# Cross-attention in a decoder layer: each unit's products on 64 columns of the tensor engine put side by side

## The chip, the cores and the metric

The kernel runs on one core of a Trainium2 chip. The core has a tensor engine (PE, with its own weight loads, PEld), a vector engine (DVE), a scalar engine (ACT), GpSimd (POOL) and a queue engine that issues most DMAs (SP). Each engine works through its own instructions strictly in the order in which they stand in its queue; engines wait for each other by semaphores. The metric is the device time of one execution in microseconds, the median of the timed runs; lower is better.

## What is computed

The reference is one decoder layer on x of 16 x 64 tokens by 256, in float32: three blocks, each added to x after a LayerNorm. The first is self-attention with block-scaled four-bit weights, the third a mixture of 16 experts with a shared expert. The change lies in the second, cross-attention against a context of 16 x 64 x 64 (16 batches, 16 heads, keys and values kept as 64 latent values):

```python
q_hk  = (hidden_q @ Wq.T).reshape(B, S, H, K)              # H = 16 heads, K = 128
q_big = einsum('bshk,hkq->bshq', q_hk, w_kc_q)             # 192 wide
q_big = _apply_rope(q_big, sin_q, cos_q)                   # rotated queries
kv_r  = _apply_rope(kv_c, sin_k, cos_k)
q_r   = einsum('bshq,hqr->bhsr', q_big, W_qr)              # 64 wide
k_r   = einsum('bld,hdr->bhlr', kv_r, W_kr)
attn  = softmax(einsum('bhsr,bhlr->bhsl', q_r, k_r))
ctx_c = einsum('bhsl,bld->bhsd', attn, kv_r)               # 64 wide
ctx   = einsum('bhsd,hkd->bhsk', ctx_c, w_kc_kv)
out   = ctx.reshape(B, S, H * K) @ Wo.T
```

## The kernel before

Products of weights are folded ahead of use (the function quad_steps, four heads, a "quad", at a time): Wq with w_kc_q into w_q (L431), W_qr with W_kr into w_s (L453), w_kc_kv with Wo into w_o (L470). With these, cross-attention has four products for each unit. A unit is one quad of heads for one half (512) of the tokens, so there are eight of them, in the list units. For each unit:

1. rotated_queries is a generator with three steps, t0, t1 and t2. A step makes two tiles of 128x512 in PSUM by w_q, each of six products with split operands (L104, tiles mm<-xn,w_q). DVE multiplies each tile by two tables of the rotation (L980, rt), and POOL adds or subtracts the results (L986, roped, two per step).
2. pair_queries multiplies the six roped tiles by w_s (L1001). Each product uses 64 of the array's 128 columns; there are twelve, written into two tiles of PSUM, one for each pair of heads. ACT copies these to q_r (L1012). A float32 product shows as two passes in the trace, so twelve products are 24 passes.
3. pair_scores multiplies q_r of one pair with the context (L1024, eight products on 64 columns, kv_bd holds two heads' keys side by side) and starts softmax: DVE takes the maximum (L324), subtracts it (L326), ACT takes the exponential (L327), DVE sums and inverts (L329, L330), and POOL scales (L334, pn). For the last unit DVE scales too.
4. transposed turns pn on PE (L343) and ACT copies it to pt (L351, L352).
5. pair_context multiplies pt with the context (L1037, eight products on 64 columns for each pair); ACT and DVE split the result into c_t (L112, L113).
6. cross_project multiplies c_t by w_o (L104, mm<-w_o,c_t, four tiles of 128x256) and DVE adds the result to x (L1062).

The loop over n interleaves three units: in iteration n unit n is rotated (items 1), unit n-1 gets its queries and scores (2 and 3), and unit n-2 its context and projection (4 to 6). Folding of quads 2 and 3 (late, in iterations 1 and 3) runs between, and so do LayerNorm's transposes (L216) in iterations 0 and 6, the router's products (choose, L793 and L794), and in the last iteration the first products of the third block.

The order in an engine's queue is not that of the code. A scheduler takes the program in the code's order as a priority and places each instruction by its own estimate of when its operands are there, so that products of different steps come to stand between one another. Two means hold it: tc.issue_after(ins) and the helper after(...) put what is traced inside them behind a given instruction in the queue of its engine, without a wait; behind(read, writes) makes an instruction wait, by semaphore, for a list of others on other engines.

[...] The pool ps_mm gives four rotating tiles, which the rotated queries, pair_queries, the folding and cross_project share: a new tile waits until DVE or ACT has read the one four places before. Scores and transposes rotate over two tiles (at), contexts and others over two (av). roped tiles are single, rt tiles double.

Of the kernel before, what the change touches and what calls it, by code (L numbers as in the profile page):

```python
# [71 lines left out]
def decoder_layer(ctx: ExitStack, tc: tile.TileContext, a: dict, out: bass.AP):  # L72
    nc = tc.nc
# [11 lines left out]
    def mm_tile(rows=128, cols=512):  # L85
        return ps_mm.tile([128, 512], F32, tag="mm", name="mm")[:rows, :cols]
# [7 lines left out]
    @contextmanager  # L94
    def after(*instructions):

        with ExitStack() as order:
            for ins in instructions:
                order.enter_context(tc.issue_after(ins))
            yield  # L100

    def matmuls(ps, pairs):
        for n, (l, r) in enumerate(pairs):
            m = nc.tensor.matmul(ps, lhsT=l, rhs=r, start=(n == 0), stop=(n == len(pairs) - 1))  # L104
        return m.ins
# [143 lines left out]
    def behind(read, writes):  # L249
        for w in writes:  # L250
            tc.add_manual_dep(
                read,
                w.name,
                mybir.DependencyInfo(mybir.DependencyClass.Sync, mybir.DependencyReason.DATA),
                reason="it reads rows of each",
            )
# [58 lines left out]
    with ExitStack() as attn:  # L315
# [4 lines left out]
        def softmax(sc, scale, eng=None):  # L320

            shape = [128, 8, S]
            m = small.tile([128, 8], F32, tag="sm_m", name="sm_m")
            nc.vector.tensor_reduce(m, sc, AX.X, ALU.max)  # L324
            p = soft.tile(shape, F32, tag="p", name="p")
            nc.vector.tensor_tensor(p, sc, m.unsqueeze(2).broadcast_to(shape), ALU.subtract)  # L326
            exps.append(nc.scalar.activation(p, p, AF.Exp, scale=scale).ins)  # L327
            s = small.tile([128, 8], F32, tag="sm_s", name="sm_s")
            nc.vector.tensor_reduce(s, p, AX.X, ALU.add)  # L329
            nc.vector.reciprocal(s, s)  # L330
            pn = soft.tile(shape, F32, tag="pn", name="pn")
            softened.append(
                (eng or nc.vector)
                .tensor_tensor(pn, p, s.unsqueeze(2).broadcast_to(shape), ALU.mult)  # L334
                .ins
            )
            return pn
# [143 lines left out]
        weights, quad_loads = {}, []  # L481
# [9 lines left out]
        with tc.tile_pool(name="sw", bufs=2, side="right") as sw, tc.tile_pool(name="sa", bufs=2, side="right") as sa:  # L491
# [121 lines left out]
            vs, qks, pns, os = {}, {}, {}, {}  # L613
# [15 lines left out]
            for h in range(NH + 3):  # L629
# [9 lines left out]
                pt = transposed(pns.pop(h - 2)) if 0 <= h - 2 < NH else None  # L639
# [315 lines left out]
        with (  # L955
# [6 lines left out]
            def rotated_queries(w_q, half, roped):  # L962
                for t in range(3):
                    m = []
                    for ab in range(2):
                        ps = mm_tile()
                        cols = slice(t * 128, (t + 1) * 128)
                        pairs = []
                        for c in range(2):
                            pairs += three(  # L970
                                [w[:, c, ab, cols] for w in w_q],
                                [p[:, c, :] for p in xn_t[half]],
                            )
                        matmuls(ps, pairs)
                        ps3 = ps.rearrange("p (b s) -> p b s", s=S)
                        for k in range(2):
                            mt = xa.tile(
                                [128, 8, S], F32, tag=f"rt{ab}{k}", name=f"rt{ab}{k}"
                            )
                            nc.vector.tensor_tensor(mt, ps3, rope_table(t, 2 * ab + k), ALU.mult)  # L980
                            m.append(mt)
                    for ab, (one, two, op) in enumerate(
                        ((m[0], m[3], ALU.subtract), (m[2], m[1], ALU.add))
                    ):
                        r = xa.tile([128, 512], F32, tag=f"roped{t}{ab}", name=f"roped{t}{ab}", bufs=1)
                        nc.gpsimd.tensor_tensor(  # L986
                            r.rearrange("p (b s) -> p b s", s=S), one, two, op
                        )
                        roped.append(r)
                    yield  # L990

            def pair_queries(w_s, roped):
                ps = [mm_tile() for _ in range(2)]
                left = [4 if h in (1, 2) else 2 for h in range(4)]
                first = [True] * 4
                for t in range(3):
                    for ab in range(2):
                        for blk in range(2):
                            h = BLOCK_HEADS[t][blk]
                            left[h] -= 1  # L1000
                            nc.tensor.matmul(  # L1001
                                ps[h // 2][(h % 2) * 64 : (h % 2) * 64 + 64],
                                lhsT=w_s[:, t, blk, ab, :],
                                rhs=roped[2 * t + ab],
                                start=first[h],
                                stop=left[h] == 0,
                            )
                            first[h] = False
                q_rs = []
                for pr in range(2):  # L1010
                    q_r = xa.tile([128, 512], F32, tag="q_r", name="q_r", bufs=2)
                    nc.scalar.copy(q_r, ps[pr])  # L1012
                    q_rs.append(q_r)
                return q_rs

            def pair_scores(q_r, half, eng):

                sc = at_tile([128, 8, S])
                sc4 = sc.rearrange("p (h g) s -> p h g s", h=2)
                for g in range(2):  # L1020
                    for pp in range(2):
                        for par in range(2):
                            b = 4 * g + 2 * par + pp
                            nc.tensor.matmul(  # L1024
                                sc4[par * 64 : par * 64 + 64, :, 2 * g + pp, :],
                                lhsT=q_r[:, b * S : (b + 1) * S],
                                rhs=kv_bd[:, half * 8 + b],
                                start=True,
                                stop=True,
                            )  # L1030
                return softmax(sc, 1.0, eng)

            def pair_context(pt, half):
                av = av_tile()
                for k in range(4):
                    for hp in range(2):
                        nc.tensor.matmul(  # L1037
                            av[hp * 64 : hp * 64 + 64, k * 128 : (k + 1) * 128],
                            lhsT=kv[:, half * 4 + k, :],
                            rhs=pt[:, 4 * hp + k].rearrange("p a q -> p (a q)"),  # L1040
                            start=True,
                            stop=True,
                        )
                c_t = [
                    xa.tile([128, 512], F32R, tag=f"c_t{n}", name=f"c_t{n}", bufs=4)
                    for n in range(2)
                ]
                parts_of(av, c_t[0], c_t[1])
                return c_t

            def cross_project(w_o, c_ts, half, last):
                for k in range(4):
# [68 lines left out]
            units = [(0, 0), (1, 0), (0, 1), (2, 0), (3, 0), (1, 1), (2, 1), (3, 1)]  # L1121
            late = {1: quad_steps(2, weights, xb), 3: quad_steps(3, weights, xw)}
            prep = iter(())
            roped, pns = {}, {}
            for n in range(len(units) + 2):
                here = range(len(units))
                if n in late:
                    prep = late[n]
# [3 lines left out]
                rotate = iter(rotated_queries(weights[qd][0], half, roped[n]) if n in here else ())  # L1132
                pts_n = [transposed(pn) for pn in pns.pop(n - 2, ())]
                if n - 1 in here:
                    q_rs = pair_queries(weights[units[n - 1][0]][1], roped.pop(n - 1))
                c_ts = [pair_context(pt, units[n - 2][1]) for pt in pts_n]
                next(rotate, None)
                if n - 1 in here:

                    eng = nc.gpsimd if n < len(units) else nc.vector  # L1140
                    pns[n - 1] = [pair_scores(q_rs[0], units[n - 1][1], eng)]
                if n in late:
                    next(prep)
                next(rotate, None)
                if n == 0:
                    with tc.issue_after(highs[-1]), tc.issue_after(lows[-1]):
                        xn_t += layernorm_t(2, (1,))
                if n - 1 in here:
                    pns[n - 1].append(pair_scores(q_rs[1], units[n - 1][1], eng))
                if n in late:  # L1150
                    next(prep)
                if n - 2 in here:
# [364 lines left out]
```

## Time and profile before

| | us |
|---|---|
| median of 3 timed runs (lowest, highest) | 567.59 (567.42, 567.69) |
| the profiled execution, its own time | 574.92 |
| its span, first to last instruction | 573.2 |
| busy in the span: PE, PEld | 539.9, 446.9 |
| busy in the span: DVE, ACT, POOL | 402.5, 278.9, 229.6 |
| mean granted clock of PE | 0.978 |

In rows of the timeline the fields are start and length in us, engine, line, operation, tiles written and read, the part of the array (rows*columns for PE), shapes and count; in brackets stands the idle time of the engine before, with what ended it. The end of a matmul is modelled, and the next one starts before it: the pace of PE is read from starts. In windows each engine has its busy time in the stretch and its number of instructions, followed by the granted clock, the DMA share and GB/s.

### The profile page before, as it was taken

Reading aid. Unit: us, or ns where it says so; the run is one execution under the profiler, and the core shown is the slowest. Engines: PE = TensorE matmul, PEld = TensorE weight load, DVE = VectorE, ACT = ScalarE, POOL = GpSimd, SP = SyncE. Lnnn points to the kernel's source line nnn. Section 1 sums busy time; section 2 is a strip of 40 time slices with the busy share of each in tenths; the row PEclk is TensorE's granted clock in tenths of the full one; section 3 lists DMA queues with packets and bytes.
Section 4 is the critical chain, followed back from the end, with each engine's and each line's share of the span. In section 5 each row is a group of like instructions: output and inputs, shape, how many; then the busy total and the mean of one; then the engine's idle time right before and its main releaser. Section 6 shows DMA issues by size and latency. Waiting matters only on the chain.

```text
span 573.2 us, 10602 instructions
## 1 busy us (share of the span) xinstructions
PE 539.9 (94%) x4013; PEld 446.9 (78%) x4013; DVE 402.5 (70%) x879; ACT 278.9 (49%) x524; POOL 229.6 (40%) x213
## 2 busy tenths in 40 slices
PE   7999999999999989999999999999999869999962
PEld 6889898888989875757777577685787769999961
DVE  5465566645655789848667486889768589999876
ACT  4767557575574431230432323152535277777551
POOL 4260500101001005526244343632545726888872
PEclk9999999999999999999999999999999789999995
DMA  8563331823200599471020000000511667777384
GB/s 244 143 189 118 105 111 45 226 82 112 75 1 1 169 249 305 131 233 44 2 70 1 8 1 1 0 31 0 189 50 69 204 197 254 243 245 241 120 283 151
DMA packets 44262, 70.83 MB, mean 124 GB/s; under 512 B 11824, under 2 KB 25232, under 8 KB 44208
## 3 DMA queue, kind: packets, MB, share of 16 engines
q1 hardware_dynamic: 39376, 58.71, 34.3%
q0 software_dynamic: 3696, 10.36, 4.7%
q10 hardware_dynamic: 1136, 1.05, 0.6%
q8 instruction: 33, 0.54, 0.4%
q14 instruction: 21, 0.17, 0.1%
HBM read 48.61 MB, written 21.86 MB: 123 GB/s over the span
## 4 chain that ended last, share of the span: by engine, by line


## 5 line engine op out<-in xcount | busy, mean ns | idle before, releaser
L986 POOL TENSOR_TENSOR roped<-rt,rt 128x512 f32<-128x512 f32 x48 | 62.7, 1327 | 82.5 <-DVE rt L980 80.2
L980 DVE TENSOR_TENSOR rt<-mm,rope_q 128x512 f32<-128x512 f32 x96 | 61.5, 684 | 23.7 <-PE mm L104 23.0
L104 PE MATMUL mm<-xn,w_q 128*128 128x512 f32 x288 | 74.2, 403 | 0.5 <-ACT xn L222 0.5
L104 PEld LDWEIGHTS mm<-xn,w_q 128*128 128x128 f32 x288 | 52.1, 188 | 14.3 <-issue 2.6
L104 PE MATMUL mm<-xs,w 128*128 128x384 f32 x270 | 55.5, 355 | 6.2 <-ACT xs L112 5.1
L1300 POOL DMA_INDIRECT yd<-y,to x45 | 48.2, 1071 | 27.3 <-ACT y L1295 12.8
L104 PEld LDWEIGHTS mm<-xs,w 128*128 128x128 f32 x270 | 48.7, 199 | 8.1 <-ACT xs L112 5.9
L327 ACT ACTIVATE p<-p 128x512 f32<-128x512 f32 x32 | 20.1, 630 | 61.9 <-DVE p L326 61.9
L1001 PE MATMUL mm<-roped,w_s 128*64 128x512 f32 x192 | 46.3, 601 | 0.0
L324 DVE TENSOR_REDUCE sm_m<-at 128x8 f32<-128x512 f32 x32 | 21.8, 680 | 34.9 <-PE at L569 34.0
L514 POOL TENSOR_TENSOR wv<-code,scale 128x512 fp32r<-128x512 f32 x7 | 9.0, 1283 | 90.1 <-DMA scale<-in_scales 55.4
L609 DVE TENSOR_TENSOR x<-mm,x 128x256 f32<-128x256 f32 x64 | 26.0, 419 | 23.9 <-PE mm L104 22.7
L104 PE MATMUL mm<-wo,o 128*128 128x256 f32 x256 | 39.6, 295 | 0.0
L104 PE MATMUL mm<-xn,wk 128*128 128x512 f32 x128 | 35.3, 406 | 0.0
L104 PE MATMUL av<-w,hp 128*128 128x256 f32 x225 | 34.9, 289 | 0.3 <-ACT y L1295 0.3
L104 PE MATMUL mm<-wv,xn 128*128 128x256 f32 x256 | 34.7, 288 | 0.0
L586 PE MATMUL av<-pt,v 128*128 128x128 f32 x256 | 34.5, 277 | 0.0
L104 PE MATMUL mm<-xn,wq 128*128 128x512 f32 x128 | 34.4, 404 | 0.0
L104 PEld LDWEIGHTS mm<-wo,o 128*128 128x128 f32 x256 | 32.9, 190 | 1.5 <-issue 0.4
L586 PEld LDWEIGHTS av<-pt,v 128*128 128x128 f32 x256 | 32.0, 191 | 1.2
L104 PEld LDWEIGHTS mm<-wv,xn 128*128 128x128 f32 x256 | 31.7, 189 | 0.7
L104 PEld LDWEIGHTS av<-w,hp 128*128 128x128 f32 x225 | 30.3, 189 | 1.3 <-ACT y L1295 0.6
(216 smaller groups left out, 1148.7 us busy)
## 6 DMA issues: line engine op xcount, KB each, us to landing
w<-in_W SPq DMA_DIRECT2D x15, 640.0 KB
code<-in_codes SPq DMA_DIRECT2D x32, 256.0 KB
scale<-in_scales SPq DMA_DIRECT2D x32, 256.0 KB
xr<-xd SPq DMA_DIRECT2D x15, 408.0 KB
xd<-zeros SPq DMA_DIRECT2D x8, 720.0 KB
yd<-zeros SPq DMA_DIRECT2D x8, 512.0 KB
got<-yd SPq DMA_DIRECT2D x16, 256.0 KB
wq<-in_Wq SPq DMA_DIRECT2D x4, 512.0 KB
```

The costliest lines, as they stand in the source:

```text
L104: m = nc.tensor.matmul(ps, lhsT=l, rhs=r, start=(n == 0), stop=(n == len(pairs) - 1))
L324: nc.vector.tensor_reduce(m, sc, AX.X, ALU.max)
L327: exps.append(nc.scalar.activation(p, p, AF.Exp, scale=scale).ins)
L514: mults[n] = eng.tensor_tensor(w, *loaded[gr].pop(n), ALU.mult).ins
L586: nc.tensor.matmul(av[:, k * 128 : (k + 1) * 128], lhsT=v[:, i, k0 : k0 + HD], rhs=pt[:, i].rearrange("p a q -> p (a q)"), start=True, sto ...
L609: nc.vector.tensor_tensor(x[i], ps, x[i], ALU.add)
L980: nc.vector.tensor_tensor(mt, ps3, rope_table(t, 2 * ab + k), ALU.mult)
L986: nc.gpsimd.tensor_tensor(r.rearrange("p (b s) -> p b s", s=S), one, two, op)
L1001: nc.tensor.matmul(ps[h // 2][(h % 2) * 64 : (h % 2) * 64 + 64], lhsT=w_s[:, t, blk, ab, :], rhs=roped[2 * t + ab], start=first[h], stop=l ...
L1300: sent = nc.gpsimd.indirect_dma_start(out=yd[: (E - 1) * SLOTS + min(TOPK, E - 1 - e) * NT], out_offset=bass.IndirectOffsetOnAxis(ap=to[:, ...
```

## The change

One unit's products on 64 columns are put in one row of PE's queue: the twelve of pair_queries, then the contexts of both pairs of the unit ahead, then the scores of both pairs. For that:

- rotated_queries yields the last product of the step, and pair_queries, pair_context and pair_scores return theirs; each next group is traced inside after(...) of the last product of the one before.
- The first step (t0) of unit n now comes ahead of pair_queries of unit n-1; the second (t1) comes behind the scores of both pairs.
- roped_last keeps the last two rotations traced; their list is passed by roped_done, and the first product of pair_queries waits for both (behind), where before each product waited for its own operand alone.
- The folding steps of late quads move behind the scores.

No product, copy or DMA is added or left out. In the lines of the changed file L1001 becomes L1004, L1012 becomes L1017, L1024 becomes L1029, L1037 becomes L1042, and L1062 becomes L1067.

```diff
@@ rotated_queries
-                        matmuls(ps, pairs)
+                        asked = matmuls(ps, pairs)
...
-                        nc.gpsimd.tensor_tensor(
+                        rotated = nc.gpsimd.tensor_tensor(
                             r.rearrange("p (b s) -> p b s", s=S), one, two, op
                         )
                         roped.append(r)
-                    yield
+                        roped_last[ab] = rotated.ins
+                    yield asked
@@ pair_queries
-                            nc.tensor.matmul(
+                            products.append(
+                                nc.tensor.matmul(
...
+                behind(products[0], roped_done.pop())
...
-                return q_rs
+                return q_rs, products[-1]
@@ pair_scores, pair_context: the last product is returned too
-                return softmax(sc, 1.0, eng)
+                return softmax(sc, 1.0, eng), last.ins
...
-                return c_t
+                return c_t, last.ins
@@ the loop over units
+            roped_last, roped_done = [None, None], []
             for n in range(len(units) + 2):
...
                 pts_n = [transposed(pn) for pn in pns.pop(n - 2, ())]
                 if n - 1 in here:
-                    q_rs = pair_queries(weights[units[n - 1][0]][1], roped.pop(n - 1))
-                c_ts = [pair_context(pt, units[n - 2][1]) for pt in pts_n]
-                next(rotate, None)
+                    roped_done.append(list(roped_last))
+                order = [m for m in [next(rotate, None)] if m]
                 if n - 1 in here:
-
-                    eng = nc.gpsimd if n < len(units) else nc.vector
-                    pns[n - 1] = [pair_scores(q_rs[0], units[n - 1][1], eng)]
-                if n in late:
-                    next(prep)
-                next(rotate, None)
+                    with after(*order):
+                        q_rs, product = pair_queries(
+                            weights[units[n - 1][0]][1], roped.pop(n - 1)
+                        )
+                    order = [product]
+                c_ts = []
+                for pt in pts_n:
+                    with after(*order):
+                        c_t, product = pair_context(pt, units[n - 2][1])
+                    order = [product]
+                    c_ts.append(c_t)
                 if n == 0:
                     with tc.issue_after(highs[-1]), tc.issue_after(lows[-1]):
                         xn_t += layernorm_t(2, (1,))
                 if n - 1 in here:
-                    pns[n - 1].append(pair_scores(q_rs[1], units[n - 1][1], eng))
+
+                    eng = nc.gpsimd if n < len(units) else nc.vector
+                    pns[n - 1] = []
+                    for q_r in q_rs:
+                        with after(*order):
+                            pn, product = pair_scores(q_r, units[n - 1][1], eng)
+                        order = [product]
+                        pns[n - 1].append(pn)
+                if n in late:
+                    next(prep)
+                with after(*order):
+                    next(rotate, None)
                 if n in late:
                     next(prep)
                 if n - 2 in here:
```

More of the change, by code (lines that the diff above doesn't have):

```diff
@@ L989, in rotated_queries @@
                         roped.append(r)
-                    yield
+                        roped_last[ab] = rotated.ins
+                    yield asked
             def pair_queries(w_s, roped):
-                ps = [mm_tile() for _ in range(2)]
+                ps, products = [mm_tile() for _ in range(2)], []
                 left = [4 if h in (1, 2) else 2 for h in range(4)]
@@ L1000, in pair_queries @@
                             left[h] -= 1
[L1001 to L1006, printed above, removed]
+                            products.append(
+                                nc.tensor.matmul(
+                                    ps[h // 2][(h % 2) * 64 : (h % 2) * 64 + 64],
+                                    lhsT=w_s[:, t, blk, ab, :],
+                                    rhs=roped[2 * t + ab],
+                                    start=first[h],
+                                    stop=left[h] == 0,
+                                ).ins
                             )
                             first[h] = False
+                behind(products[0], roped_done.pop())
                 q_rs = []
@@ L1023, in pair_scores @@
                             b = 4 * g + 2 * par + pp
-                            nc.tensor.matmul(
+                            last = nc.tensor.matmul(
                                 sc4[par * 64 : par * 64 + 64, :, 2 * g + pp, :],
@@ L1036, in pair_context @@
                     for hp in range(2):
-                        nc.tensor.matmul(
+                        last = nc.tensor.matmul(
                             av[hp * 64 : hp * 64 + 64, k * 128 : (k + 1) * 128],
```

## The prediction

> **What bounds the kernel now.** I read the page first (span, busy time by engine, slices), then the windows by stage, then the tensor engine's timeline through one unit of the stage that the change touches, then the waits, and last the stretches behind it where the tensor engine pauses.
>
> ```profile
> span 573.2 us, 10602 instructions
> PE 539.9 (94%) x4013; PEld 446.9 (78%) x4013; DVE 402.5 (70%) x879; ACT 278.9 (49%) x524; POOL 229.6 (40%) x213
> ...
> PEclk9999999999999999999999999999999789999995
> ```
>
> The profiled execution took 574.92 us, 1.7 more than its span; the median of the timed runs is 567.59. I sum differences against the profiled one and carry them over unchanged. What a measurement of this kernel can tell from no change is about 0.2%, 1.1 us.
>
> ```profile
> 336.00:358.00 22.00, 22.00 (x160) 15.57 (x159) 16.35 (x29) 7.40 (x12) 11.13 (x9) 1.00 0.01 1
> ```
>
> The columns are stretch, length, then busy time of PE, PEld, DVE, ACT and POOL. In cross-attention (about 214 to 419 us) PE has work without a break while VectorE is busy three quarters and GpSimd half of the time: PE's queue sets the pace. Busy PE is not all products, though, as one unit shows:
>
> ```profile
> 335.36 3.13 PE L104 MATMUL mm<-w_o,c_t 128*128 128x256 f32 x24
> 338.32 2.96 PE L104 MATMUL mm<-xn,w_q 128*128 128x512 f32 x12
> 341.21 3.71 PE L1001 MATMUL mm<-roped,w_s 128*64 128x512 f32 x16
> 344.85 0.66 PE L343 MATMUL at<-ident,pn 128*128 128x128 f32 x4
> 345.26 1.64 PE L104 MATMUL mm<-xn,w_q 128*128 128x512 f32 x6
> 346.74 0.60 PE L343 MATMUL at<-ident,pn 128*128 128x128 f32 x4
> 347.10 2.35 PE L104 MATMUL mm<-xn,w_q 128*128 128x512 f32 x9
> 349.37 1.94 PE L1001 MATMUL mm<-roped,w_s 128*64 128x512 f32 x8
> 351.14 1.92 PE L1037 MATMUL av<-pt,kv 128*64 128x128 f32 x32
> 352.88 1.04 PE L1024 MATMUL at<-kv_bd,q_r 128*64 128x128 f32 x16
> 353.86 2.37 PE L104 MATMUL mm<-xn,w_q 128*128 128x512 f32 x9
> 356.16 1.09 PE L1024 MATMUL at<-kv_bd,q_r 128*64 128x128 f32 x16
> ```
>
> Each row gives start, length, source line, tiles and the part of the array used: 128*64 are the products on 64 columns. They stand in three groups here (from 341.21, 349.37 and 356.16), with 128-column work between.
>
> **The saving.** The cost of one excursion to 64 columns, from these rows: twelve xn passes at 0.233 ((2.96 less the last pass's 0.40, over 11) are 2.80, but 338.32 to 341.21 is 2.89: 0.09 on entering. The L1024 group entered from 128 columns takes 1.09, the one entered from 64 columns 1.04: 0.05. That group lasts 0.98 to the next start (352.88 to 353.86), where 16 of the 32 L1037 passes take 0.87 (1.74 / 2): 0.11 on leaving. And the xn group right behind takes 0.1 longer (331.33 to 334.33 is 3.00 against 2.89). Sum 0.35 us. The waits say the same of the weight loads:
>
> ```profile
> PEld mm L1001 <- issue: 20.5, 73, 0.4
> ```
>
> Counted in the timeline there are 34 such groups between 223 and 412 us; in the changed program's PE queue 16 remain: one for each of the eight iterations with queries, three split again (four w_q products of L431 come between the first unit's queries and scores, eight transposes in iteration 7, L793 and L794 twice in iteration 8), three for the weight steps L453 and L470, one for the last context. 18 x 0.35 = **6.3 us saved**. No product is added or dropped; the DMA issues on SP's queue keep their order.
>
> **What is moved, and what it now waits for.** PE's queue becomes, per unit: t1 (second of three rotations, 12 xn passes a pair of tiles), w_o x18 (passes of L104), transposes A, w_o x6, t2, t0 of the next unit, transposes B, 24 L1001 passes, 32 context, 32 score, all in order. Before, the first 16 L1001 passes needed only t0 and t1, and stood in PE's queue as cover while VectorE and GpSimd rotated t2. Now the explicit wait holds even the first L1001 for the last rotated tile; queued behind it are contexts, scores, the next t1, and with them VectorE's softmax. The cover left is t0 of the next unit (2.8) and transposes (0.45).
>
> An ordinary unit, clock 0 at t1, with durations of the trace (VectorE 0.60 from one 128x512 operation to the next, 0.71 where it needs the one before; x additions 0.33; GpSimd below):
>
> ```profile
> 364.10 1.26 DVE L980 TENSOR_TENSOR rt<-mm,rope_q 128x512 f32<-128x512 f32 x2
> 364.90 2.50 POOL L986 TENSOR_TENSOR roped<-rt,rt 128x512 f32<-128x512 f32 x2 [2.81 <-DVE rt L980]
> ...
> 344.49 1.94 POOL L986 TENSOR_TENSOR roped<-rt,rt 128x512 f32<-128x512 f32 x1
> ```
>
> Both scores now end together, so VectorE gets both softmaxes at once, behind the second c_t. sm_m A starts at -0.45, sm_s A at 2.2, the two t1a products 2.8 to 4.0, reciprocal A 4.0, sm_s B 4.1, t1b products end at 6.0. GpSimd's pn A (1.04) runs 4.3 to 5.3, so transposes A start at 5.4 where PE was there at 5.05; the fourth w_o tile needs t1b's PSUM buffer (four rotate) and starts at 6.05 instead of 5.5: 0.55 lost. t2 then ends at 9.6, t0 at 12.4, transposes B at 12.85. VectorE takes t2b 0.35 after its last pass started, GpSimd begins after the third product, at 10.55, and needs 2.50: 13.05. The first L1001 starts at 13.1 and PE was ready at 12.95. About 0.75 lost per unit, against 2 x 0.35 saved: **an ordinary unit is even.**
>
> Unit by unit (n is the loop's iteration) the losses are: n=1: only t0 and eight LayerNorm transposes cover the first t2, whose rotation ends near 228.1 where PE is there at 226.4: 1.7. n=2: weight steps cover everything: 0. n=3: 0.75. n=4: L431 and L453 cover: 0.2. n=5: L470 covers in part: 0.4. n=6: 0.75, and the two ws splits (L113, 0.9 and 2.0 us) fall beside t2's rotation; the row at 344.49, taken beside such a split, has GpSimd at 1.94 instead of 1.25: 0.9 more. n=7: 0.75 and the LayerNorm statistics 0.25. n=8: no next unit, so no t0: t2 ends at 10.85, transposes at 11.3, rotation at 14.3 to 15.1: 3.8. In the end, w_o follows the scores directly and waits for c_t: 0.5. Sum **10.0 us**.
>
> The trace has no row of PE waiting for GpSimd's rotation. Bounds: zero (PE arrives last everywhere but at the start and in n=8; 1.7 + 3.0), and 1.4 more for each of six units if every rotation ran at 1.94 (8.4 more). I take the 1.25 rows, since most rotations (mean 1.327 of 48) are near them. The release itself is cheap: the q_r copy that ended at 392.96 let a score start at 393.02.
>
> Waits of before in this stretch that the new order doesn't have (q_r 0.6, c_t 0.6, and small ones near 402): **1.5 us back**.
>
> **The clock.** Pauses of before behind this stage:
>
> ```profile
> 449.18 1.08 PE L104 MATMUL mm<-ws,sh 96*128 96x256 f32 x4 [1.64 <-issue]
> ...
> 450.00:452.00 2.00, 1.54 (x8) 1.14 (x6) 1.98 (x5) 0.25 (x1) 1.70 (x2) 0.50 0.32 33
> ...
> 467.87 0.79 PE L104 MATMUL mm<-xs,w 128*128 128x384 f32 x3 [2.12 <-ACT xs L112]
> ...
> 470.00:472.00 2.00, 1.81 (x8) 1.80 (x8) 1.97 (x5) 1.43 (x2) 1.67 (x3) 0.50 0.69 146
> ```
>
> The granted clock (third from the right) fell to 0.50 within 2 us of pauses of 1.64 and 2.12; a third pause of 2.21 at 460 was followed by 1.00. The Trainium skill ("TensorE: Matmul & The Clock Gate", HAM oscillation) gives the rule that only idle gaps over about 3.4 us bring the half clock. By it the pauses above would have kept full clock, and of my losses only n=8's 3.8 is near. By the rows any pause of 1.6 us may. The rows decide: the half clock lasted from some 2.8 us (470 to 473) to 6.3 (450 to 456), a cost of half of that. By the rule n=8 costs 0 if its pause stays at 3.0; by the rows 1.4 to 3.1. I take **1.4**, the later row, whose pause stands in a dense queue as here.
>
> Net: 10.0 + 1.4 - 6.3 - 1.5 = +3.6 us. The end of this stage goes through: LayerNorm, routing and the sends (GpSimd's queue was waiting 5.25 us for the second half's targets) all follow the last w_o. Span 576.8, and **571.2 us** by the median.
>
> **Rivals.**
> - Faster: the rotations fit under t0 and the transposes, and only the start and n=8 pause (1.7 + 3.0), at full clock: 4.7 - 6.3 - 1.5 = -3.1, 564.5. For it: an ordinary unit misses by 0.15 at the L1001 and by 0.55 at w_o, and the excursions are measured. Against it: two places per unit have to fit. It decides when the pauses sum to less than 7.8.
> - No change: pauses of 7 to 9 us without the half clock: about 567.6.
> - Much slower: two softmaxes in a row keep VectorE behind by a unit's third, GpSimd meets it, rotations take 1.94: +8.4, 579.6. For it: pn now sits between t1's and t2's rotations in GpSimd's queue. Against it: only SBUF-to-SBUF operations stretched GpSimd so far.
> - That the change leaves the groups apart is excluded by the queue, apart from the splits counted above.
>
> **Numbers.** Forecast (569 to 575) 0.45, faster 0.25, no change 0.13, much slower 0.17. So faster 0.25, same 0.13, slower 0.62. The range 564 to 578 leaves out the ends of the two outer cases; the forecast's own is 569 to 575.
>
> **What would show it.** Right: L1001 rows of x24 in one group; about 18 fewer groups; PE waiting for POOL roped at L1001 some 7 to 9 us in all, longest in iteration 8; PE at transposes or w_o waiting for pn or DVE; a dip of the clock near 390 to 400. Wrong: no PE wait on roped in the middle units (then it is faster), or waits over 2 us in each (then it is much slower), or excursions that cost less than 0.35 when there are few of them.

## The result, and the profile after

| | before | after |
|---|---|---|
| median of the timed runs (lowest, highest), us | 567.64 (567.42, 569.24) | 573.84 (571.51, 574.45) |
| the profiled execution, its own time, us | 574.92 | 571.51 |
| its span, us; mean granted clock | 573.2; 0.978 | 569.7; 0.985 |

The change makes the kernel slower by 6.2 us, ratio 1.0097 with a 95% interval of 1.0068 to 1.0125. The two profiled executions alone would say the opposite (574.92 and 571.51): that of before met two stretches of half clock (the clock granted to PE fell to 0.50) in the expert stage, near 449 to 456 and 470 to 473, and that of after, which is also the fastest of its four runs, met none there. So spans are not compared here. What is compared is the cross-attention stage, from the first w_q product (214.2 us in both) to the start of the last w_o product: 204.8 us before, 209.8 after.

The page of after, first its span and busy times, then the granted clock in 40 slices:

```profile
span 569.7 us, 10601 instructions
PE 531.8 (93%) x4013; PEld 442.6 (78%) x4013; DVE 405.2 (71%) x879; ACT 279.3 (49%) x524; POOL 229.1 (40%) x213
...
PEclk9999999999999999999999999998999999999995
```

As many PE instructions as before, and one slice of this stage below 9 (the 28th, at 385 to 399). The timeline of PE through two units, iterations 6 and 7 of the loop:

```profile
344.33 0.60 PE L343 MATMUL at<-ident,pn 128*128 128x128 f32 x4
345.80 5.37 PE L1004 MATMUL mm<-roped,w_s 128*64 128x512 f32 x24 [0.86 <-POOL roped L986]
351.00 1.92 PE L1042 MATMUL av<-pt,kv 128*64 128x128 f32 x32
352.74 1.92 PE L1029 MATMUL at<-kv_bd,q_r 128*64 128x128 f32 x32
...
357.49 2.30 PE L104 MATMUL mm<-w_o,c_t 128*128 128x256 f32 x18
360.05 0.66 PE L343 MATMUL at<-ident,pn 128*128 128x128 f32 x4 [0.26 <-POOL pn L334]
...
368.16 5.37 PE L1004 MATMUL mm<-roped,w_s 128*64 128x512 f32 x24 [0.48 <-POOL roped L986]
...
373.95 0.60 PE L216 MATMUL av<-ident,wkq 128*128 128x128 f32 x4
375.74 1.97 PE L1042 MATMUL av<-pt,kv 128*64 128x128 f32 x32 [1.18 <-DVE xn L224]
```

An ordinary unit has one row of 64-column products, L1004, L1042, L1029, and the 128-column order around it is the one the prediction wrote down. In brackets is what the new order brought: PE waits for GpSimd's last rotation and for GpSimd's pn. In iteration 7 the row is split, and the contexts' PSUM tile waits until VectorE has read LayerNorm's transposes (L216); the program has these at the end of iteration 6, and in PE's queue they stand right ahead of the contexts. The last unit, iteration 8:

```profile
387.37 2.95 PE L104 MATMUL mm<-xn,w_q 128*128 128x512 f32 x12
390.16 0.60 PE L343 MATMUL at<-ident,pn 128*128 128x128 f32 x4
394.56 7.07 PE L1004 MATMUL mm<-roped,w_s 128*64 128x512 f32 x24 [3.81 <-POOL roped L986]
401.56 0.43 PE L793 MATMUL av<-sel,upto 128*128 128x64 f32 x2
```

With no next unit there is no t0 to cover the rotation, and PE stands for 3.81 us. The row behind lasts 7.07 instead of 5.37, and the windows there (the granted clock stands third from the right) say why:

```profile
394.00:396.00 2.00, 1.44 (x6) 0.54 (x8) 1.83 (x15) 0.00 (x0) 0.51 (x1) 0.77 0.03 8
396.00:398.00 2.00, 2.00 (x8) 0.59 (x6) 1.66 (x13) 0.00 (x0) 0.00 (x0) 0.50 0.00 0
398.00:400.00 2.00, 2.00 (x10) 0.62 (x8) 0.00 (x0) 0.00 (x0) 0.00 (x0) 0.88 0.00 0
```

The half clock lasted 3.4 us, so 1.7 us were lost: 7.07 - 5.37. The longest waits of PE from 214 to 424 us, with their sum, their number and the longest one:

```profile
PE mm L1004 <- POOL roped L986: 5.4, 4, 3.8
PE av L216 <- DVE ln_x L192: 1.6, 2, 1.0
PE av L1042 <- DVE xn L224: 1.2, 1, 1.2
PE at L343 <- POOL pn L334: 1.0, 4, 0.3
```

### The profile page after: what moved, and what is told of

It is laid out like the page before. It is cut to its first block, busy times and chain, and to the rows that moved or that the text cites. A ratio compares the mean times of both kernels' runs of the same rounds, so it can differ in the third digit from the quotient of the medians.

```text
span 569.7 us, 10601 instructions
## 1 busy us (share of the span) xinstructions
PE 531.8 (93%) x4013; PEld 442.6 (78%) x4013; DVE 405.2 (71%) x879; ACT 279.3 (49%) x524; POOL 229.1 (40%) x213
## 4 chain that ended last, share of the span: by engine, by line
## 5 line engine op out<-in xcount | busy, mean ns | idle before, releaser
L104 PE MATMUL mm<-xn,w_q 128*128 128x512 f32 x288 | 72.1, 400 | 0.5 <-ACT xn L222 0.5
L104 PE MATMUL mm<-xs,w 128*128 128x384 f32 x270 | 53.0, 342 | 4.9 <-ACT xs L112 2.7
L104 PEld LDWEIGHTS mm<-xs,w 128*128 128x128 f32 x270 | 45.8, 188 | 7.1 <-ACT xs L112 3.8
L1004 PE MATMUL mm<-roped,w_s 128*64 128x512 f32 x192 | 44.7, 616 | 5.4 <-POOL roped L986 5.4
L351 ACT COPY pt<-at 64x512 f32<-64x512 f32 x32 | 18.5, 577 | 43.3 <-PE at L343 42.8
L334 POOL TENSOR_TENSOR pn<-p,sm_s 128x512 f32<-128x512 f32 x14 | 14.6, 1043 | 62.0 <-DVE sm_s L330 62.0
L1004 PEld LDWEIGHTS mm<-roped,w_s 128*64 128x64 f32 x192 | 13.8, 140 | 31.4 <-issue 23.4
```

The lines of the kernel that those rows point to most:

```text
L351: nc.scalar.copy(pt[:S, :, 0, :], ps[:S])
L1004: nc.tensor.matmul(ps[h // 2][(h % 2) * 64 : (h % 2) * 64 + 64], lhsT=w_s[:, t, blk, ab, :], rhs=roped[2 * t + ab], start=first[h], stop=l ...
```

## The experiments

Theory A is the prediction's account: fewer switches between 64 and 128 columns save time, and the explicit wait for the last rotation, with the half clock behind its longest pause, costs more than that. Theory B is in each case the rival that the expectation names.

**The wait left out, in one iteration or in all.** All of these change one line, the list handed to behind(); without it each product of pair_queries waits for its own operand alone, as before the change.

```diff
-                    roped_done.append(list(roped_last))
+                    roped_done.append(list(roped_last) if n < len(units) else [])        # e1_last_free
+                    roped_done.append([])                                                # e2_no_hold
+                    roped_done.append(list(roped_last) if n > 1 else [])                 # e7_first_free, e10
+                    roped_done.append(list(roped_last) if 1 < n < len(units) else [])    # e8_middle_hold
```

Without it in iteration 8 (e1):

> The changed kernel, but in iteration 8, where no next unit's t0 covers the rotation, the first L1004 no longer waits for the last rotated tile: eight products run beside it. Theory A (the biggest part of the loss is the pause of 3.8 us there and the half clock behind it, about 1.7 us on 24 passes at 0.84 instead of 0.43 per pair): both go, two excursions to 64 columns come back (0.7), so 4 to 5 us less than the changed kernel: 568.5 to 570. Theory B (the pause only moves, since sel of the router or the last context then ends last): 1 to 2 us less, 572 or more.

Measured 570.47 (568.11 to 572.39), ratio 1.0051 (1.0033 to 1.0069): 3.4 us less than after, and not the 4 to 5 of theory A. The trace of e1 in iteration 8, and PE's waits behind it:

```profile
387.54 2.96 PE L104 MATMUL mm<-xn,w_q 128*128 128x512 f32 x12
390.42 3.71 PE L1004 MATMUL mm<-roped,w_s 128*64 128x512 f32 x16
394.07 0.66 PE L343 MATMUL at<-ident,pn 128*128 128x128 f32 x4
394.76 1.94 PE L1004 MATMUL mm<-roped,w_s 128*64 128x512 f32 x8
```
```profile
PE mm L104 <- DVE x L1067: 1.2, 1, 1.2
PE at L343 <- DVE r_p L878: 0.4, 1, 0.4
PE mm L104 <- ACT c_t L112: 0.3, 1, 0.3
```

Sixteen of the 24 passes need only t0 and t1, and run while the rotation of t2 is under way. The pause of 3.8 us is gone, and the clock stayed at 1.00 in the stage. But 1.9 us of waits come up behind it, where after has 0.1: in part theory B is right, the pause moves. So 3.8 + 1.7 - 1.8 = 3.7 are won, less one more group, and the stage is 3.2 us shorter.

Without it anywhere (e2):

> The changed kernel without the explicit wait in any iteration (each product waits for its own operand alone); the groups stay together in iterations 2, 4 to 6, split in 1, 3 and 8. Theory A: as with the wait gone in iteration 8 alone, and 1 to 2 us less from iterations 1, 6 and 7: 567 to 569. Theory B (the wait is harmless but in iteration 8, the order itself costs): the same as with iteration 8 alone, within 0.5.

Measured 566.37 (565.33 to 568.14), ratio 0.9979 (0.9971 to 0.9987): below the range of theory A, and faster than before by 0.2%. An ordinary unit of it (iteration 6):

```profile
343.29 0.60 PE L343 MATMUL at<-ident,pn 128*128 128x128 f32 x4
343.82 5.43 PE L1004 MATMUL mm<-roped,w_s 128*64 128x512 f32 x24
349.03 1.97 PE L1042 MATMUL av<-pt,kv 128*64 128x128 f32 x32
350.77 1.97 PE L1029 MATMUL at<-kv_bd,q_r 128*64 128x128 f32 x32
```

The row is as long as in after and starts right behind the transposes: the products whose operands are there cover those that are not. What is left are waits that the wait on the rotation has no part in, the second as in e1:

```profile
PE at L343 <- POOL pn L334: 1.2, 5, 0.3
PE mm L104 <- DVE x L1067: 1.2, 1, 1.2
PE av L1042 <- DVE xn L224: 1.2, 1, 1.2
```

Without it in iteration 1 alone (e7, and again as e10 on another chip):

> The changed kernel without the explicit wait in iteration 1 alone; two more 64-column groups form there. Theory A: the two pauses of iteration 1 (1.24 and 0.89 us, LayerNorm's transposes and behind them) go, less two excursions of 0.35, and the half clock behind them (seen in one of three profiles with these pauses, at 229 to 233 us, worth 1.9 us) with them: 1.4 to 3.3 us under the changed kernel's 573.84, so 570.5 to 572.4. Theory B (the pause is LayerNorm's own and stays, since VectorE delivers ln_x no earlier): 573 to 574.5.

> The run without the wait in iteration 1 once more (570.67, ratio 1.0053, on another chip), as the partner of the next one: the run with idle work in the pause of iteration 8 was on a chip on which the kernel before took 570.82, 3.2 us more than elsewhere. Both theories: ratio 1.004 to 1.007.

Measured 570.67 (ratio 1.0053, 1.0034 to 1.0071) and 569.92 (1.0037, 1.0023 to 1.0052). In both traces the pauses at L216 are gone, 1.6 us, for two more groups. With the half clock of iteration 8 set aside, their stages are 1.8 us shorter than that of after. By the ratios the medians fell by 2.5 and 3.4 us, with an interval of some 2 us on either side, so more than 1.8 is not shown. What can hang on these pauses besides shows in two executions that have them. The windows of after and of the run e4 below at 228 to 234:

```profile
228.00:230.00 2.00, 1.38 (x9) 0.61 (x10) 2.00 (x4) 0.98 (x2) 0.45 (x1) 1.00 0.99 271
230.00:232.00 2.00, 2.00 (x12) 0.65 (x10) 2.00 (x4) 0.10 (x1) 0.84 (x1) 1.00 1.04 272
232.00:234.00 2.00, 2.00 (x12) 0.58 (x8) 0.19 (x1) 0.59 (x1) 1.67 (x2) 1.00 0.98 251
```
```profile
228.00:230.00 2.00, 1.38 (x8) 0.54 (x8) 2.00 (x4) 0.85 (x2) 0.59 (x1) 0.94 1.03 278
230.00:232.00 2.00, 2.00 (x6) 0.49 (x4) 2.00 (x4) 0.23 (x1) 0.70 (x1) 0.50 1.00 260
232.00:234.00 2.00, 2.00 (x10) 0.72 (x8) 0.32 (x1) 0.00 (x0) 1.79 (x2) 0.71 0.89 236
```

The pauses are 0.97 and 0.62 us in the one and 0.96 and 0.62 in the other. In after (and in e1) the clock stayed full. In e4 it fell to 0.50 for 3.4 us, and the first w_o product came 1.9 us later (265.2 against 263.3), of which 0.1 was there at the start of the stage. A pause is not always followed by the half clock.

With the wait in iterations 2 to 7 alone (e8):

> The changed kernel with the explicit wait in iterations 2 to 7 alone, none in iterations 1 and 8. Theory A (the two ends make the loss, and they add up): 573.84 - 3.4 (what leaving out iteration 8's wait saved) - 3.2 (iteration 1's) = 567.2; 566.5 to 568.2, within about 1 us of the run without any explicit wait (566.37). Theory B (each wait in the middle costs 0.4 to 0.75 us, as the prediction's sum had it, 2.9 us in all from iteration 3 to 7): 569 to 570.

Measured 572.60, on a chip on which before took 570.82; the ratio is 1.0034 (1.0022 to 1.0046), as much as 569.6 against 567.64. That is theory B's number, yet not by theory B's way. Up to the first w_o product of iteration 8 its trace is 1.0 us behind e2's (182.8 against 181.8 us from the first w_q product). The rest comes later, from a transfer that was issued late. SP's issue of it and the row of ACT that cuts these weights, those of the last expert, first in e2 and then in e8, and the longest wait of PE in e8 behind 395 us:

```profile
402.31 0.33 SPq L1083 DMA_DIRECT2D w_last_down<-in_W  x1
404.93 0.62 ACT L112 CAST w_last<-w_last_down 128x512 fp32r<-128x512 f32 x1 [1.63 <-DMA w_last_down<-in_W]
```
```profile
404.84 0.33 SPq L1083 DMA_DIRECT2D w_last_down<-in_W  x1
407.51 0.62 ACT L112 CAST w_last<-w_last_down 128x512 fp32r<-128x512 f32 x1 [2.79 <-DMA w_last_down<-in_W]
```
```profile
PE at L343 <- DVE r_p L878: 1.4, 1, 1.4
```

From issue to cut it took 2.6 us in e2 and 2.7 in e8. But SP issued it in e2 when the w_o product that reads its buffer had ended (402.28), and in e8 1.2 us behind that (403.64). So ACT waited 1.16 us longer, VectorE's half of the cut stands ahead of the last pn in its queue, and PE's transposes waited 1.4 us instead of the 0.4 of e2. What held SP is not shown; the run e9 below, on the same chip, has no such delay (it and its twin e11 on another chip cut these weights 194.4 and 194.3 us after the first w_q product). So the middle waits cost 1.0 us by the trace, and about 3 at most by the ratio (1.0034 against e2's 0.9979).

**The new order in the middle alone.** Iterations 0, 1, 7, 8 and 9 have the order of before, 2 to 6 the new one, with the wait (e5) and without it (e6).

```diff
+                if 2 <= n <= 6:
                     ...                       # the new order; in e6 with roped_done.append([])
+                else:
+                    if n - 1 in here:
+                        roped_done.append([])
+                        q_rs, _ = pair_queries(...)
+                    c_ts = [pair_context(pt, units[n - 2][1])[0] for pt in pts_n]
+                    next(rotate, None)
                     ...                       # scores of the first pair, late step, t2, scores of the second
```

> The new order and its wait in iterations 2 to 6 alone, the order of before in iterations 0, 1, 7, 8 and 9. Theory A (the middle iterations are even: two excursions saved against 0.75 us of waits, more saved beside the weight steps; the loss lies at the start and in iterations 7 and 8): 566 to 569, within 0.3% of before. Theory B (every iteration of the new order loses about a fifth of the whole): 570 to 572.

> The new order in iterations 2 to 6 alone, and without the explicit wait for the last rotation there; iterations 0, 1, 7 and 8 have the order of before. Theory A (the wait costs little in the middle, where t0 and the transposes cover the rotation): 0 to 1 us under the run with the wait (567.75), so 566.8 to 567.8. Theory B (the wait costs 0.4 to 0.75 us in each of these iterations, as the prediction's sum had it, 2.3 us in all): 565 to 566.

Measured 567.75 (ratio 1.0004, 0.9992 to 1.0016) and 566.97 (0.9988, 0.9978 to 0.9997). With the wait the middle is even, as forecast for "an ordinary unit"; leaving it out is worth 0.8 us there by the medians and 0.4 in the traces' stages, hardly more than the noise. The loss of the whole change lies at its ends, in iterations 1, 7 and 8.

**The price of an excursion.** Two twins of after: one short product ahead of each rotated tile, on 64 columns (e3a) or on 128 (e3b).

```diff
+                        nc.tensor.matmul(ps[:64, :64], lhsT=ident[:, :64], rhs=ident[:, :64], ...)   # e3a
+                        nc.tensor.matmul(ps[:, :64], lhsT=ident, rhs=ident[:, :64], ...)             # e3b
                         asked = matmuls(ps, pairs)
```

> The changed kernel with 48 short products added, one ahead of each rotated tile's six products, on 64 columns (64x64 by 64x64, into the tile's PSUM, which the first of the six products overwrites). Its output is that of the changed kernel. To be read against the run with the same 48 products on 128 columns; eight of the 48 stand right behind a 64-column group, the other 40 are excursions of their own inside 128-column work. Theory A, the prediction's 0.35 us for an excursion: 40 x 0.35 = 14 us over the 128-column twin, a few us less where an excursion falls beside a pause (11 to 14). Theory B, an excursion costs little (0.1 us, about what a short pass takes anyway): 4 us or less over the twin.

> The twin: the same 48 short products in the same places, on 128 columns (128x128 by 128x64). Its output is that of the changed kernel. Both theories: the passes' own time alone, 96 passes at 0.03 to 0.06 us, 3 to 6 us over the changed kernel's 573.84, so 577 to 580.

Measured 583.75 (583.15 to 583.99) and 578.84 (577.33 to 579.31), so 4.9 us apart, near B's number and far from A's 14. But the medians do not give the price. In e3b PE stands longer in the stage (6.6 us, in e3a 5.0), the half clock behind the pause of iteration 8 lasts 6.8 us instead of 3.4, and three of its four executions have a mean clock of 0.978 or 0.979, where e3a's have 0.984 and 0.985. The price is read from the sites. One of each in the trace, e3a and then e3b:

```profile
302.61 0.33 PE L974 MATMUL mm<-ident 128*64 128x64 f32 x2
302.87 1.67 PE L104 MATMUL mm<-xn,w_q 128*128 128x512 f32 x6
304.46 0.33 PE L974 MATMUL mm<-ident 128*64 128x64 f32 x2
```
```profile
299.95 1.64 PE L104 MATMUL mm<-xn,w_q 128*128 128x512 f32 x6
301.43 0.33 PE L974 MATMUL mm<-ident 128*128 128x64 f32 x2
301.57 1.64 PE L104 MATMUL mm<-xn,w_q 128*128 128x512 f32 x6
```

A short product and the six passes take 1.85 us on 64 columns (302.61 to 304.46) and 1.62 on 128 (299.95 to 301.57): 0.23 for the excursion. The 27 sites behind a w_q pass cost 0.22 to 0.24 each, and so do 11 behind transposes, w_o products or L431 (0.21 to 0.24). Six that stand behind a 64-column group cost 0.12 less than the twin, which changes columns there. All sites of the stage come to 8.0 us, and the two stages differ by 8.0 when idle time and half clock are taken off. So the price is 0.23, neither A's 0.35 nor B's 0.1.

Its parts: the pass ahead of the short product is followed 0.09 later (327 ns, with 128 columns 234), the first w_q pass comes 0.12 later (258 and 139), and the second 0.02 (335 ns after the first, and 315). Where a w_q pass follows another it is 232, so the twin is no free base: most of the prediction's "0.1 longer" behind an excursion belongs to the seam between two kinds of products, whatever columns they use.

**The half clock of iteration 8.** Idle work in the pause: 30 transposes of the identity (e4, on after), or six products on 64 columns (e9 and again e11, on e7).

```diff
                 ps, products = [mm_tile() for _ in range(2)], []
+                if fill:                                   # in iteration 8 alone
+                    with after(pn_turned[0]):
+                        for k in range(fill):              # e4: 30 times
+                            nc.tensor.transpose(ps[0][:, ...], ident, ident)
+                        ...                                # e9, e11: three times both halves of the columns
+                            nc.tensor.matmul(ps[0][...], lhsT=w_s[:, 0, 0, 0, :], rhs=roped[0], ...)
```

> The changed kernel with 30 transposes of the identity (30 x 0.108 = 3.2 us of PE work) put into the pause of iteration 8, behind the transposes of pn; the wait itself stays. Theory A (the pause of 3.8 lets the clock fall to half, which costs 1.7): clock 1.00 there, L1004 passes at 0.43 a pair, 1.3 to 2 us less than the changed kernel. Rival (the products at half clock end no later, since sel or c_t end last): no difference within 0.5. A pause that the filler lengthens would make it slower by up to 1.

> The changed kernel without the wait in iteration 1, and with idle work in the pause of iteration 8: six more products on 64 columns (a rotated tile by w_s, both halves of the columns, into the PSUM tile that the first true product overwrites), 12 passes of 0.24 us, 2.9 of the 3.8 us. Its output is that of the changed kernel. To be read against the run with the same queue and no idle work (570.67), so that only the half clock behind the pause can differ. Theory A (the half clock follows the pause, 3.4 us long in one profile and 6.1 in another, and costs half of that): 1.7 to 3 us less, 567.7 to 569. Theory B (the idle work costs what it saves, as the transposes in the earlier run seemed to): 570 to 572.

> The same with the six idle products on 64 columns in the pause of iteration 8, now on the same chip as its partner. Theory A (the half clock behind that pause is in most executions, and the profile's 3.0 us less at the end of the stage come through): 1.5 to 3 us less than the partner. Theory B (what the idle work saves in the stage is lost behind it, or the timed executions seldom have the half clock there): within 1 us of the partner, or above it.

Measured: e4 575.35 (ratio 1.0132, 1.0114 to 1.0150); e9 575.06 on the chip on which before took 570.82 (1.0078, 1.0054 to 1.0101); e11 569.50 (1.0036, 1.0027 to 1.0045) beside its partner e10 with 569.92 (1.0037). In the stage the work does what theory A says. PE's rows of e10 and then of e11:

```profile
393.14 7.07 PE L1004 MATMUL mm<-roped,w_s 128*64 128x512 f32 x24 [3.80 <-POOL roped L986]
400.14 0.43 PE L793 MATMUL av<-sel,upto 128*128 128x64 f32 x2
```
```profile
389.22 2.80 PE L1000 MATMUL mm<-roped,w_s 128*64 128x512 f32 x12
391.85 6.65 PE L1015 MATMUL mm<-roped,w_s 128*64 128x512 f32 x24
398.43 0.43 PE L793 MATMUL av<-sel,upto 128*128 128x64 f32 x2
```

The row ends 1.7 us earlier, which is the cost of a half clock of 3.4 us, although PE did 2.8 us more work. (It is 6.65 long because three passes on one half of the columns ran ahead while the other half still waited.) The profiled executions differ by 1.8 (570.41 and 568.61). The medians differ by 0.4, too little to be told from no change. So the half clock of iteration 8 is seen in each profile that has the unfilled pause, and its price in the stage is shown; that the median falls by as much is not. In the timed runs the median of the mean granted clocks was 0.983 with the pause and 0.985 with the idle work, so some of it may have come through. Why not all, and why e4 and e9 came out above their partners, stays open. e4's profile met the half clock in iteration 1 and two stretches of it in the expert stage besides, which its idle work has no part in. e9's stage is as long as that of e11, the same kernel (206.3 in both), so what it lost lies behind the stage.

## Why the prediction held, and which of its terms were off

The mechanism held: fewer groups saved time, the wait at the head of the row and the half clock behind its longest pause cost more. One sum fits, within 0.7 us, all kernels to which no work was added. For each profile: the 64-column groups in PE's queue, its idle times of 0.1 us and more, the cost of half clock in the stage (half its length, as far as PE worked in it), and the length of the stage; last, the length less idle time and half clock.

| | groups | idle | half clock | stage | rest |
|---|---|---|---|---|---|
| before | 33 | 1.6 | 0 | 204.8 | 203.2 |
| e6 | 22 | 3.8 | 0 | 204.4 | 200.6 |
| e5 | 21 | 4.9 | 0 | 204.8 | 199.9 |
| e2 | 20 | 4.3 | 0 | 203.9 | 199.6 |
| e8 | 19 | 7.9 | 0 | 207.2 | 199.3 |
| e1 | 17 | 7.5 | 0 | 206.6 | 199.1 |
| e7 | 18 | 8.0 | 2.8 | 209.1 | 198.3 |
| e10 | 18 | 8.0 | 1.7 | 208.0 | 198.3 |
| after | 16 | 9.5 | 1.7 | 209.8 | 198.6 |

- *The groups* fell to 16, as counted; before has 33 in its trace, not 34, so 17 went. *Their price* was mis-sized: the rest fell by 4.6 us, 0.27 for a group instead of 0.35, and the twins say 0.23. The failed term is the 0.1 that the following w_q passes take longer: it was put down to the columns, and the twin on 128 columns has most of it too. Where a group goes, other products meet, and the likely reason is that they pay at that seam. The idle time of the weight loads at L1001, 20.5 us in 73 waits, was no second witness: it stands between the passes inside a group, about 0.3 each time, and with half of the groups gone it is 23.4 us in 79 waits. Saved 4.6, not 6.3.
- *The losses* came to 9.5 us against 10.0; that the sum is so near is in part luck. By iteration, forecast and idle time measured: n=1 1.7 and 1.6; n=2 0 and 0.3; n=3 0.75 and 0.4; n=4 0.2 and 0.3; n=5 0.4 and 0.3; n=6 1.65 and 1.1; n=7 1.0 and 1.7; n=8 3.8 and 3.8; the end 0.5 and 0.1. Their places were not all right. In n=1 PE stands at LayerNorm's transposes, not at L1004. In n=3 to 5 L1004 waits 0.2 or not at all, and what is left are transposes that wait for pn or a w_o tile. So the waits for roped at L1004 are 5.4 us in all, below the 7 to 9 that the prediction named as a sign. And n=7 has 1.18 that the prediction did not have: the contexts' PSUM tile, held by VectorE's read of LayerNorm's transposes. This wait is in e2 too, so it comes from the new order and not from the explicit wait.
- *The waits of before* (1.5) were won back: 1.6 us of idle time there, and in after none in those places but at L216.
- *The half clock of iteration 8* was 1.7 us against the 1.4 taken, which had been read from windows of 2 us; in windows of 1 us that row's stretch lasts 3.4 us as well (and the longer one 6.8, not 6.3). On the rule weighed there, that only pauses over about 3.4 us bring it, iteration 8 decides nothing, since its pause is longer. Iteration 1 speaks against it: pauses of 0.97 and 0.62 us were followed by 3.4 us of half clock in one profile out of three. The prediction was right to put the rows above the rule; what the rows did not say is that it is a matter of the execution.
- *The sum in the stage* is then 9.5 + 1.7 - 4.6 - 1.6 = 5.0 us, where the prediction had 3.6.
- *That the end of the stage goes through to the end* held: LayerNorm's last ln_rstd on GpSimd came at 426.1 against 421.5, 4.6 later; in e2 it came 1.0 earlier and in e1 1.6 later, with medians 1.5 below and 2.6 above before. For after that leaves about 1.2 us of the 6.2. They go with the clock: the three runs of after that were not profiled had 573.7 to 574.5 us at mean clocks of 0.978 to 0.982, the profiled one 571.51 at 0.985, and before has a median of 0.984 in the later runs. An estimate from the medians of the clocks, 0.0025 of 570 us, is 1.4. Where this half clock lies is not shown, since no trace of those runs exists. Iteration 1 is a candidate, by e4; but e7, which has no pause there, ran at a median of 0.9805 too.
- *The rivals*: the faster one needed pauses under 7.8 us in all and missed that by the wait's own share, as e2, with 4.3, shows: with 20 groups it is faster than before (0.9979). The much slower one did not come: GpSimd took 3.28 us for the last two rotations of iteration 8 and 3.17 for those of iteration 6, where VectorE cuts weights beside it, and 2.50 to 2.54 for those of the other middle iterations.

## What to carry to other kernels

Putting like products in a row saves at each seam, here a quarter of a microsecond a group. What it cost here was not the row but the wait at its head, which asked for more than its first operand. A head that waits for everything takes away the work that covered the last operand, most of all where the pipeline runs out and no next unit stands beside it. Let each product wait for its own operand and keep the row by queue order alone, and look at the first and last trips of the loop apart from the middle ones.

## What the runs showed of the hardware that was not expected

- A change to 64 columns and back costs 0.23 us of PE's time in the midst of 128x512 passes (27 sites, 0.22 to 0.24), against the same short product on 128 columns. That product costs about 0.08 besides its own time at the seam to the 512-wide ones (315 ns against 232).
- The half clock comes in stretches of one length. In windows of 1 us every stretch ahead of the kernel's tail lasts 3.4 us (such as before at 470, after, e2, e4, e8, e10) or twice that: 6.8 in before at 450, and in e7, from 392.1 to 398.9, at the same pause of 3.8 us that was followed by 3.4 in after and e10. The same pauses of 0.97 and 0.62 us were followed by it in one of three executions. So one profile shows whether the half clock can come at a pause, not how often.
